# Pooling a CIN kernel's sums over the partitions: four column groups of the array in place of one

## The chip, the cores and the metric

The kernel runs on one core of one Trainium2 chip. The metric is the device time in microseconds; lower is better. The page of the profile shows one execution by itself, whose span runs from its first instruction to its last. Engines go by these names: PE is TensorE (PEld its weight loads), DVE is VectorE, ACT is ScalarE, POOL is GpSimd, SP is SyncE, which here issues transfers only.

## The reference

The input is a batch of 1024 rows, each with 64 fields of 16 numbers. Three layers of a compressed interaction network follow, each a product of every field of the input with every field of the layer before, contracted with a weight matrix; then the sums over the 16 numbers, and one dot product:

```python
for i in range(n):                                   # n = 3
    z = jnp.einsum('bfe,bge->bfge', x0, h)
    z = z.reshape(Bn, f0 * fh, e)
    y = jnp.einsum('oc,bce->boe', Ws[i], z) + bs[i][None, :, None]
    x_i, h = (y[:, :half, :], y[:, half:, :])        # the last layer: (y, y)
    xs.append(x_i)
pooled = jnp.sum(jnp.concatenate(xs, axis=1), axis=2)
return pooled @ fc_w.T + fc_b
```

The result is one number for each row of the batch, 1024 in all.

## The kernel before, in words

The batch is cut into 32 chunks of 32 rows; a chunk has 512 columns (row times number). The final dot product is folded into the weights, so that only two kinds of terms are left for each chunk: a product of two contracted sums (`factors`), and a product of the input with a linear form of it (`x_v0x`). Both are written to a tile `uu`; `sums` has VectorE add each run of 16 columns and puts the result into `acc`, a tile of [128, 2, 16, 32]: 128 partitions, two kinds of sums, 16 pairs of chunks (`NP` is 16), 32 rows of the batch. The even chunk of a pair lies in partitions 0 to 63, the odd one in 64 to 127. What is left is a sum over those 64 partitions and over the two kinds, with a bias added. That is the pooling.

The order of the work is written out by hand, and each engine runs its own instructions in that order. VectorE makes the products `z` (`product`, line 223) from loads that SP issues, TensorE contracts them with the weights (`contract`, line 257; `half_contract`, line 291, for the first four chunks), ScalarE copies half of a contracted sum (line 361), and VectorE multiplies and reduces (lines 362 and 371). Each chunk takes 16 matmuls of 128x128 weights by 512 columns. The last chunk is contracted in two pieces of 256 columns each, with the pooling placed within the second piece, after two of its four groups of four matmuls (lines 699 to 704).

Pooling (lines 630 to 634) is a matmul with `ones`, two columns of weights: one has ones in the upper 64 partitions, the other in the lower 64. So the result `po` has two partitions, one for the even and one for the odd chunks. For the first 15 pairs there are two matmuls of 480 columns, one for each kind, added up in PSUM; for the last pair there are two of 32 columns, the second of which comes after the last sums. `finish` (lines 636 to 638) has ScalarE add the bias `cst` on the way to SBUF and issues a transfer to the output on ScalarE's queue.

The bias is made near the start: lines 196 to 201 multiply the folded weights with the biases of the layers, in two accumulating matmuls of one column whose weights are a column repeated twice, and line 398 adds the last bias in ScalarE. The result has two partitions. Around it stand a few matmuls on zeros[...] (`keep_clock`, line 105), the shifted copies of the input for the first chunks (line 184), and the first contraction.

Of the kernel before, what the change touches and what calls it, by code (L numbers as in the profile page):

```python
# [36 lines left out]
F32 = mybir.dt.float32  # L37
AF = mybir.ActivationFunctionType
ALU = mybir.AluOpType
# [3 lines left out]
E = 16  # L43
B = 1024
CB = 32
# [17 lines left out]
def cin_kernel(ctx, tc, xra, xrb, wh, w0r, w1h, w2t, wx1, wx0, vec, out):  # L63
    nc = tc.nc
# [6 lines left out]
    ps = ctx.enter_context(tc.tile_pool(name="ps", bufs=2, space=bass.MemoryType.PSUM))  # L71
# [3 lines left out]
    def const_tile(name, shape):  # L75
        return const.tile(shape, F32, tag=name, name=name)
# [12 lines left out]
    vs = const_tile("vs", [128, NV])  # L89
    nc.scalar.dma_start(out=vs, in_=vec)  # L90
    fc2, bh1, bh2 = vs[:, 0:1], vs[:, 1:2], vs[0:64, 2:3]
    bcol, fcol, fcb = vs[:, 3:5], vs[:, 5:7], vs[0:2, 7:8]
    w0ds, fcr = vs[:, 8:72], vs[:, 72:200]

    fv2 = const_tile("fv2", [128, 32])
# [5 lines left out]
    misc = ps.tile([128, N], F32, tag="acc", name="misc", bufs=4)  # L101
# [9 lines left out]
    for base in (0, 64, -64):  # L111
        nc.gpsimd.affine_select(
            out=shift, in_=shift, compare_op=ALU.not_equal, fill=1.0, base=base,
# [3 lines left out]
    ones = const_tile("ones", [128, 2])  # L117
# [75 lines left out]
    keep_clock(3)  # L193


    cst = const_tile("cst", [2, 1])
    for j in range(2):
        nc.tensor.matmul(
            misc[0:2, 0:1], fcol[:, j : j + 1].to_broadcast([128, 2]), bcol[:, j : j + 1],
            start=(j == 0), stop=(j == 1),  # L200
        )


    acc = const_tile("acc", [128, 2, NCH // 2, CB])
# [14 lines left out]
    def product(c, j, first=0, last=NI, engine=nc.vector):  # L219
        if first == 0:  # L220
            zs[c, j] = z_tile(f"z_{c}_{j}")
        at = slice(first, last)
        engine.tensor_tensor(  # L223
            zs[c, j][:, at, :], xas[c][:, at, :],
            xbs[c][j].unsqueeze(1).to_broadcast([128, last - first, N]), ALU.mult,
        )
        if j == NJ - 1:
            nc.scalar.activation(zs[c, j][SQ, 0, :], xas[c][SQ, 0, :], AF.Square)  # L228
# [24 lines left out]
    def contract(c, j, piece=0):  # L253
        acc_c, cols = pieces(c)[piece]
        for i in tiles(j):
            t = j * NI + i
            nc.tensor.matmul(  # L257
                acc_c, w_all[:, t, w_cols(c)], zs[c, j][:, i, cols],
                start=(t == 0 and c % 4 < 2), stop=(t == NT - NI and c % 4 >= 2),
            )  # L260
# [90 lines left out]
    def factors(c, which=slice(0, 1)):  # L351

        uu = uu_tile(c // 2)[halves[c % 2], 0, :]
        if c in HEAD:
            at = halves[1 - c % 2]
            nc.vector.tensor_tensor(uu, q_accs[c // 2][at], hb[at, c // 2, :], ALU.mult)
            return
        h = halves[c % 2]
        for acc_c, cols in pieces(c)[which]:
            q = sp.tile([128, N], F32, tag="q", name=f"q_{c}_{cols.start}")  # L360
            nc.scalar.copy(q[h, cols], acc_c[64 - h.start : 128 - h.start])  # L361
            nc.vector.scalar_tensor_tensor(  # L362
                uu[:, cols], acc_c[h], bh1[h], q[h, cols], ALU.add, ALU.mult
            )
# [4 lines left out]
    def sums(k, rows=slice(0, 128), of=slice(0, 2), half=slice(0, CB)):  # L369

        nc.vector.tensor_reduce(  # L371
            acc[rows, of, k, half],
            uus[k][rows, of, E * half.start : E * half.stop].rearrange("p k (b e) -> p k b e", e=E),
            AX.X,
            ALU.add,
        )
# [18 lines left out]
    nc.scalar.copy(w0o[0], w0s[0][:, :, 1, :])  # L395
    h1_weights(0, w0o[0])
    product(c0, 0, 2, NI)
    nc.scalar.activation(cst, misc[0:2, 0:1], AF.Identity, bias=fcb, scale=float(E))
    nc.scalar.copy(w0o[1], w0s[1][:, :, 1, :])
    product(c0, 2)  # L400
    h1_weights(1, w0o[1])
# [31 lines left out]
    for n in range(2):  # L433
        pv = ps.tile([128, 512], F32, tag=("y", "set")[n], name=f"pv2_{n}")
        for k in range(4):
            nc.tensor.matmul(  # L436
                pv[32 * k : 32 * k + 32], fv2, w2s[n][:, k * 512 : (k + 1) * 512],
                start=True, stop=True,
                tile_position=(0, 32 * k),
# [5 lines left out]
    for h in range(2):  # L445
        at = slice(32 * h, 32 * h + 32)
# [30 lines left out]
    def m_ap(f1, f2, dims):  # L477
        return bass.AP(tensor=md.tensor, offset=md.offset + f1 * row + f2 * F, ap=dims)
# [3 lines left out]
    for half, queue in enumerate((nc.sync, nc.scalar)):  # L482
        queue.dma_start(
            out=m_ap(0, 32 * half, [[row, F], [1, 32 * F]]), in_=m_rows[halves[half]]
# [5 lines left out]
        out=m_ap(64, 68, [[row, 4], [4 * F, 7], [1, 4 * F]]),  # L490
        in_=m_rows[0:4, 4 * F :].rearrange("p (k c) -> p k c", c=4 * F),
# [132 lines left out]


    NP = NCH // 2
    res = const_tile("res", [2, NP, CB])
    outs = out.rearrange("(k h b) o -> h k (b o)", h=2, b=CB)

    def pool(pairs, part):  # L630
        nc.tensor.matmul(  # L631
            po[:, pairs, :], ones, acc[:, part, pairs, :],
            start=(part == 1), stop=(part == 0), skip_group_check=True,
        )

    def finish(pairs):
        nc.scalar.activation(res[:, pairs, :], po[:, pairs, :], AF.Identity, bias=cst)
        nc.scalar.dma_start(out=outs[:, pairs, :], in_=res[:, pairs, :])


    order = [4, 5, 6, 7, 2, 3] + list(range(8, NCH))
    first, last = slice(0, NP - 1), slice(NP - 1, NP)
    for s, c in enumerate(order):
        k, head = c // 2, c in HEAD
        if 0 < s < len(order) - 2 and s not in (2, 3):
# [43 lines left out]
            x_v0x(k)  # L689
            sums(k - 1)  # L690

    po = ps.tile([2, NP, CB], F32, tag="set", name="po")


    sums(NP - 1, of=slice(1, 2))
    sums(NP - 1, slice(0, 64), slice(0, 1))
    factors(NCH - 1)
    sums(NP - 1, slice(64, 128), slice(0, 1), slice(0, CB // 2))
    for j in range(NJ):
        if j == 2:  # L700
            pool(first, 1)
            pool(first, 0)
            pool(last, 1)
        contract(NCH - 1, j, 1)
    finish(first)
    factors(NCH - 1, slice(1, 2))
    sums(NP - 1, slice(64, 128), slice(0, 1), slice(CB // 2, CB))
    pool(last, 0)
    finish(last)


# [69 lines left out]
```

## Time and profile before

Three runs took 489.01, 489.15 and 489.27 us; their median is 489.15 us. The run that was profiled took 489.07 us, and its span is 487.3 us, at a full TensorE clock.

| What (profile before) | us |
|---|---|
| span of the profiled execution | 487.3 |
| TensorE matmul busy | 482.3 |
| VectorE busy | 367.6 |
| ScalarE busy | 90.7 |
| pooling matmuls (line 631), 8 records | 2.0 |
| activation of 2x480 in `finish` | 0.65 |
| activation of 2x32 in `finish` | 0.28 |
| issue of the first and the second output transfer | 0.50 and 0.26 |

Busy time is what the records of an engine cover. The records of matmuls overlap each other and their ends are modelled, so TensorE's share says only that it nearly always had a matmul in hand. What is worth reading is the chain of work that ended last: it follows back from the last instruction to what released each step. A group line gives the program's line, the engine, the operation, the tiles written and read, the shapes and the number of records; the bracket at the end of a timeline line gives the idle time ahead of it and what ended that. An f32 matmul leaves two records of weight load and two of matmul.

### The profile page before, as it was taken

Reading aid. Unit: us, or ns where it says so; the run is one execution under the profiler, and the core shown is the slowest. Engines: PE = TensorE matmul, PEld = TensorE weight load, DVE = VectorE, ACT = ScalarE, POOL = GpSimd, SP = SyncE. Lnnn points to the kernel's source line nnn. Section 1 sums busy time; section 2 is a strip of 40 time slices with the busy share of each in tenths; the row PEclk is TensorE's granted clock in tenths of the full one; section 3 lists DMA queues with packets and bytes.
Section 4 is the critical chain, followed back from the end, with each engine's and each line's share of the span. In section 5 each row is a group of like instructions: output and inputs, shape, how many; then the busy total and the mean of one; then the engine's idle time right before and its main releaser. Section 6 shows DMA issues by size and latency. Waiting matters only on the chain.

```text
span 487.3 us, 3939 instructions
## 1 busy us (share of the span) xinstructions
PE 482.3 (99%) x1622; PEld 216.4 (44%) x1622; DVE 367.6 (75%) x229; ACT 90.7 (19%) x158; POOL 16.6 (3%) x15
## 2 busy tenths in 40 slices
PE   9999999999999999999999999999999999999996
PEld 4564344343344344444444344443444434444474
DVE  5993899998899988898777687767868676680311
ACT  3325202022211122212221112212022122010001
POOL 5340000000000000000000000000000000000000
PEclk9999999999999999999999999999999999999999
DMA  8967974442746263544333244433244440000000
GB/s 335 422 250 229 426 299 172 172 172 108 317 178 261 82 263 126 208 182 174 153 116 126 124 172 172 172 140 117 89 172 172 172 172 1 0 0 1 0 0 2
DMA packets 14386, 78.59 MB, mean 161 GB/s; under 512 B 3772, under 2 KB 4444, under 8 KB 5472
## 3 DMA queue, kind: packets, MB, share of 16 engines
q1 hardware_dynamic: 13228, 77.05, 40.1%
q10 hardware_dynamic: 1140, 1.29, 0.9%
q8 instruction: 13, 0.21, 0.2%
q14 instruction: 5, 0.04, 0.0%
HBM read 76.69 MB, written 1.64 MB: 161 GB/s over the span
## 4 chain that ended last, share of the span: by engine, by line
PE 99%; DVE 0%; ACT 0%; issue 0%; POOL 0%; POOLq 0%
PE acc L257 79%; PE acc L291 6%; PE q L330 6%; PE acc L279 3%; PE acc L267 2%; PE xp L184 1%; PE misc L105 1%; PE po L631 0%; PE pm L462 0%; PE pv L436 0%; PE q L279 0%; PE q L341 0%; PE y L284 0%; PE acc L312 0%; DVE uu L362 0%
## 5 line engine op out<-in xcount | busy, mean ns | idle before, releaser
L257 PE MATMUL acc<-z,w_all 128*128 128x512 f32 (+1 forms) x928 | 387.6, 579 | 0.0
L223 DVE TENSOR_TENSOR z<-xa,xb 128x2048 f32<-128x2048 f32 x125 | 281.0, 2285 | 45.9 <-PE acc L257 38.6
L257 PEld LDWEIGHTS acc<-z,w_all 128*128 128x128 f32 x928 | 175.4, 190 | 210.9 <-issue 208.0
L228 ACT ACTIVATE z<-xa 32x512 f32<-32x512 f32 x34 | 21.3, 625 | 324.4 <-DVE z L223 321.9
L362 DVE SCALAR_TENSOR_TENSOR uu<-acc,vs,q 64x512 f32<-64x512 f32 (+1 forms) x29 | 21.2, 731 | 59.9 <-ACT q L361 59.7
L291 PE MATMUL acc<-z,w_all 128*64 128x256 f32 x256 | 28.5, 381 | 0.0
L330 PE MATMUL q<-z,w_all 128*64 128x512 f32 x128 | 27.9, 594 | 0.0
L361 ACT COPY q<-acc 64x512 f32<-64x512 f32 (+1 forms) x29 | 16.4, 565 | 36.5 <-PE acc L257 22.9
L291 PEld LDWEIGHTS acc<-z,w_all 128*64 128x64 f32 x256 | 18.0, 137 | 11.2 <-issue 2.5
L223 DVE TENSOR_TENSOR z<-xa,xp 128x2048 f32<-128x2048 f32 (+2 forms) x10 | 18.1, 1856 | 5.9 <-PE xp L184 5.9
L371 DVE TENSOR_REDUCE acc<-uu 128x64 f32<-128x1024 f32 (+3 forms) x19 | 20.3, 1073 | 0.3
L240 ACT COPY xx<-xa 64x512 f32<-64x512 f32 x32 | 19.6, 613 | 0.5
L236 ACT ACTIVATE sq<-xa 32x512 f32<-32x512 f32 x28 | 17.6, 629 | 0.7
L330 PEld LDWEIGHTS q<-z,w_all 128*64 128x64 f32 x128 | 9.0, 137 | 18.3 <-issue 18.0
L284 PE MATMUL y<-xx,bd 64*64 64x512 f32 x64 | 15.5, 603 | 0.0
L279 PE MATMUL acc<-xx,v1w 64*64 64x512 f32 (+1 forms) x58 | 13.5, 587 | 0.0
L367 DVE SCALAR_TENSOR_TENSOR uu<-y,cx,xx 128x512 f32<-128x512 f32 x16 | 11.4, 746 | 0.3
L223 POOL TENSOR_TENSOR z<-xa,xb_gps 128x2048 f32<-128x2048 f32 x2 | 9.1, 4564 | 5.8 <-ACT xb_gps L387 4.3
L267 PE MATMUL acc<-sq,w_sq 32*128 32x512 f32 (+1 forms) x58 | 8.0, 623 | 0.0
L279 PEld LDWEIGHTS acc<-xx,v1w 64*64 64x64 f32 x58 | 3.6, 132 | 8.9 <-issue 8.8
L223 POOL TENSOR_TENSOR z<-xa,xb 128x2048 f32<-128x2048 f32 x1 | 5.9, 5890 | 13.1 <-DMA xb<-in_xrb 13.1
L184 PE MATMUL xp<-xa,shift 64*64 64x512 f32 x32 | 5.6, 803 | 0.0
(62 smaller groups left out, 65.2 us busy)
## 6 DMA issues: line engine op xcount, KB each, us to landing
xa<-in_xra SPq DMA_DIRECT2D x32, 1024.0 KB, 4.8
xb<-in_xrb SPq DMA_DIRECT2D x31, 1024.0 KB, 6.9
w<-in_w2t SPq DMA_DIRECT2D x2, 1024.0 KB, 10.9
xa<-in_xra SPq DMA_DIRECT2D x2, 768.0 KB, 7.9
w1s<-in_w1h SPq DMA_DIRECT2D x1, 1024.0 KB
w1x<-in_wx SPq DMA_DIRECT2D x1, 1024.0 KB, 9.0
w0x<-in_wx SPq DMA_DIRECT2D x1, 1024.0 KB, 7.2
w0t<-in_w0r SPq DMA_DIRECT2D x1, 768.0 KB, 6.5
```

The lines of the kernel that those rows point to most:

```text
L223: engine.tensor_tensor(zs[c, j][:, at, :], xas[c][:, at, :], xbs[c][j].unsqueeze(1).to_broadcast([128, last - first, N]), ALU.mult,)
L228: nc.scalar.activation(zs[c, j][SQ, 0, :], xas[c][SQ, 0, :], AF.Square)
L236: nc.scalar.activation(sqs[c // 4][at : at + 32], xas[c][0:32, 0, :], AF.Square)
L240: nc.scalar.copy(xxs[c // 2][to], xas[c][to, 0, :])
L257: nc.tensor.matmul(acc_c, w_all[:, t, w_cols(c)], zs[c, j][:, i, cols], start=(t == 0 and c % 4 < 2), stop=(t == NT - NI and c % 4 >= 2),)
L267: nc.tensor.matmul(acc_c, w_sq[at, w_cols(c)], sqs[first // 4][at, cols], start=(r >= 2), stop=(r < 2), tile_position=(32 * r, 0),)
L279: nc.tensor.matmul(acc_c[q], v1w[rows], xxs[k][rows, cols], start=False, stop=(c >= FIRST and c % 4 < 2), skip_group_check=True,)
L291: nc.tensor.matmul(accs[c][halves[n]], w_all[:, t, 0:64], zs[c, j][:, i, n * H2 : (n + 1) * H2], start=(t == 0), stop=False,)
L330: nc.tensor.matmul(q_accs[k][halves[1 - n]], w_all[:, t, 64:128], zs[2 * k + n, j][:, i, :], start=(t == 0), stop=False,)
L361: nc.scalar.copy(q[h, cols], acc_c[64 - h.start : 128 - h.start])
L362: nc.vector.scalar_tensor_tensor(uu[:, cols], acc_c[h], bh1[h], q[h, cols], ALU.add, ALU.mult)
L371: nc.vector.tensor_reduce(acc[rows, of, k, half], uus[k][rows, of, E * half.start : E * half.stop].rearrange("p k (b e) -> p k b e", e=E), ...
```

## The change

Ahead of the pooling, VectorE adds the two kinds of sums of the first 15 pairs in place (128 partitions by 480 numbers). The pooling of these pairs then has one matmul for each quarter of the pairs in place of one for each kind: four pairs (the last quarter three) each, with 128 or 96 columns. Each quarter goes to a column group of the array of its own, so that its result lies in partitions 0, 32, 64 or 96 and the one after it. The last pair still has two matmuls of 32 columns, now in the fourth group. `finish` is called for each quarter and for the last pair: five activations and five transfers in place of two and two, the four of the quarters on SP's queue. As the results lie in several partitions, the bias is made in all 128: the weights of the two matmuls at line 198 are a column repeated 128 times.

```diff
-    bcol, fcol, fcb = vs[:, 3:5], vs[:, 5:7], vs[0:2, 7:8]
+    bcol, fcol, fcb = vs[:, 3:5], vs[:, 5:7], vs[:, 7:8]
...
-    cst = const_tile("cst", [2, 1])
+    cst = const_tile("cst", [128, 1])
     for j in range(2):
         nc.tensor.matmul(
-            misc[0:2, 0:1], fcol[:, j : j + 1].to_broadcast([128, 2]), bcol[:, j : j + 1],
+            misc[:, 0:1], fcol[:, j : j + 1].to_broadcast([128, 128]), bcol[:, j : j + 1],
...
-    nc.scalar.activation(cst, misc[0:2, 0:1], AF.Identity, bias=fcb, scale=float(E))
+    nc.scalar.activation(cst, misc[:, 0:1], AF.Identity, bias=fcb, scale=float(E))
...
+    QP = NP // 4
-    res = const_tile("res", [2, NP, CB])
+    res = const_tile("res", [128, QP, CB])
-    def pool(pairs, part):
+    def pool(k0, k1, part=0, **flags):
+        g, at = k0 // QP, slice(k0 % QP, (k1 - 1) % QP + 1)
         nc.tensor.matmul(
-            po[:, pairs, :], ones, acc[:, part, pairs, :],
-            start=(part == 1), stop=(part == 0), skip_group_check=True,
-        )
+            po[32 * g : 32 * g + 2, at, :], ones, acc[:, part, k0:k1, :],
+            tile_position=(0, 32 * g), skip_group_check=True, **flags,
+        )
-    def finish(pairs):
-        nc.scalar.activation(res[:, pairs, :], po[:, pairs, :], AF.Identity, bias=cst)
-        nc.scalar.dma_start(out=outs[:, pairs, :], in_=res[:, pairs, :])
+    def finish(k0, k1, queue):
+        g, at = k0 // QP, slice(k0 % QP, (k1 - 1) % QP + 1)
+        rows = slice(32 * g, 32 * g + 2)
+        nc.scalar.activation(
+            res[rows, at, :], po[rows, at, :], AF.Identity, bias=cst[rows]
+        )
+        queue.dma_start(out=outs[:, k0:k1, :], in_=res[rows, at, :])
...
-    po = ps.tile([2, NP, CB], F32, tag="set", name="po")
+    po = ps.tile([128, QP, CB], F32, tag="set", name="po")
+    quarters = [(k, min(k + QP, NP - 1)) for k in range(0, NP, QP)]
...
+    done = acc[:, :, 0 : NP - 1, :]
+    nc.vector.tensor_tensor(done[:, 0], done[:, 0], done[:, 1], ALU.add)
     for j in range(NJ):
         if j == 2:
-            pool(first, 1)
-            pool(first, 0)
-            pool(last, 1)
+            for at in quarters:
+                pool(*at, start=True, stop=True)
+            pool(NP - 1, NP, 1, start=True, stop=False)
         contract(NCH - 1, j, 1)
-    finish(first)
+    for at in quarters:
+        finish(*at, nc.sync)
     factors(NCH - 1, slice(1, 2))
     sums(NP - 1, slice(64, 128), slice(0, 1), slice(CB // 2, CB))
-    pool(last, 0)
-    finish(last)
+    pool(NP - 1, NP, start=False, stop=True)
+    finish(NP - 1, NP, nc.scalar)
```

More of the change, by code (lines that the diff above doesn't have):

```diff
@@ L626, in cin_kernel @@
     NP = NCH // 2
-    res = const_tile("res", [2, NP, CB])
+    QP = NP // 4
+    res = const_tile("res", [128, QP, CB])
     outs = out.rearrange("(k h b) o -> h k (b o)", h=2, b=CB)
-    def pool(pairs, part):
+    def pool(k0, k1, part=0, **flags):
+        g, at = k0 // QP, slice(k0 % QP, (k1 - 1) % QP + 1)
         nc.tensor.matmul(
-            po[:, pairs, :], ones, acc[:, part, pairs, :],
-            start=(part == 1), stop=(part == 0), skip_group_check=True,
-        )
-    def finish(pairs):
-        nc.scalar.activation(res[:, pairs, :], po[:, pairs, :], AF.Identity, bias=cst)
-        nc.scalar.dma_start(out=outs[:, pairs, :], in_=res[:, pairs, :])
+            po[32 * g : 32 * g + 2, at, :], ones, acc[:, part, k0:k1, :],
+            tile_position=(0, 32 * g), skip_group_check=True, **flags,
+        )
+    def finish(k0, k1, queue):
[5 more added lines that the diff above has]
+        queue.dma_start(out=outs[:, k0:k1, :], in_=res[rows, at, :])
     order = [4, 5, 6, 7, 2, 3] + list(range(8, NCH))
-    first, last = slice(0, NP - 1), slice(NP - 1, NP)
     for s, c in enumerate(order):
```

## The prediction

> **What bounds the kernel now.** I read the page first: how busy the engines are, and the chain of work that ended last.
>
> ```profile
> span 487.3 us, 3939 instructions
> PE 482.3 (99%) x1622; PEld 216.4 (44%) x1622; DVE 367.6 (75%) x229; ACT 90.7 (19%) x158; POOL 16.6 (3%) x15
> ...
> PE 99%; DVE 0%; ACT 0%; issue 0%; POOL 0%; POOLq 0%
> ```
>
> The chain is TensorE nearly throughout. So a microsecond taken from TensorE's own stream shortens the run, unless another engine then comes late; work added to VectorE or ScalarE costs only where TensorE comes to wait for it. The pooling lies at the end, so I asked for the chain over the last stretch (start, length, what).
>
> ```profile
> 473.83 3.88 PE acc L257 x18
> 477.71 1.76 PE po L631 x6
> 479.47 3.67 PE acc L257 x16
> 483.14 0.02 issue
> 483.16 0.37 ACT q L361
> 483.53 0.03 issue
> 483.56 0.50 DVE uu L362
> 484.06 0.02 issue
> 484.08 0.43 DVE acc L371
> 484.51 0.14 issue
> 484.64 0.23 PE po L631 x2
> 484.88 0.02 issue
> 484.90 0.28 ACT res L637
> ```
>
> The reader is to see two things. The pooling in the middle (L631 x6) costs 1.76 us on the chain, with contraction before and behind it. From 483.14 on there is a fixed serial tail, one engine after another. The timeline of the same stretch shows who is idle around it:
>
> ```profile
> 475.22 0.42 DVE L371 TENSOR_REDUCE acc<-uu 64x16 f32<-64x256 f32 x1
> 477.64 0.09 PEld L631 LDWEIGHTS po<-acc,ones 128*2 128x2 f32 x2 [0.33 <-issue]
> ...
> 478.05 0.08 PEld L631 LDWEIGHTS po<-acc,ones 128*2 128x2 f32 x1 [0.32 <-issue]
> 478.45 0.09 PEld L631 LDWEIGHTS po<-acc,ones 128*2 128x2 f32 x1 [0.32 <-issue]
> ...
> 479.51 0.65 ACT L637 ACTIVATE res<-po,cst 2x480 f32<-2x480 f32 x1 [4.85 <-PE po L631]
> 480.19 0.50 ACTq L638 DMA_DIRECT2D out<-res  x1
> ```
>
> An f32 matmul leaves two records, and the weight loads show one pass of 480 columns each 0.40 us. VectorE is free from 475.64 to 483.56, ScalarE from 480.84 to 483.16, and SP has nothing left to issue but its wait for the last output.
>
> **What the skill says.** "TensorEngine Tiling (Array Packing)", Key Properties: different tiles of the array load weights and multiply in parallel, and a change of tiling mode drains the engine. The trace agrees. Line 436 runs eight f32 matmuls of 128x32 weights by 512 columns, in two rounds of four column groups; its weight loads:
>
> ```profile
> 17.57 0.16 PEld L436 LDWEIGHTS pv<-w,fv 128*32 128x32 f32 x8 [0.39 <-issue]
> 18.03 0.13 PEld L436 LDWEIGHTS pv<-w,fv 128*32 128x32 f32 x4 [0.30 <-issue]
> 18.45 0.13 PEld L436 LDWEIGHTS pv<-w,fv 128*32 128x32 f32 x4 [0.30 <-issue]
> ```
>
> They come in fours, 0.42 to 0.46 us apart, and the next block starts at 19.43. At the pool's rate (0.40 us per 480 columns, so 0.427 per 512) the sixteen records would take 6.83 us in a row; they took 19.43 - 17.57 = 1.86. "TensorE: Matmul & The Clock Gate", The cost: per-tile semaphore tail, gives some 26 ns for each semaphore increment after a packed group; no row here isolates it.
>
> **The change part by part.** All against the profiled span of 487.3 us; that run took 489.07 us, the three timed ones 489.01 to 489.27 (median 489.15), so a difference in the span is carried over unchanged.
>
> 1. *The middle pooling on TensorE.* Before: two matmuls of 480 columns, two passes each, 4 x 0.40 = 1.60; one of 32 columns, 2 x 32 x 0.40/480 = 0.05; the rest of 1.76, 0.11, is the change of mode. After: four matmuls of 128, 128, 128 and 96 columns in four column groups, then the one of 32 in the fourth group. If the groups run together, as in line 436: 2 passes x 128 x 0.40/480 = 0.21, plus 0.05, plus a fixed part. From line 436, 1.86 - 4 x 0.427 = 0.15. Sum 0.42. Bounds: issue alone gives 0.34, as line 198's four records with one column each took 0.17 on the chain, some 0.025 apart with 0.09 of mode change, and ten records at 0.025 plus 0.09 are 0.34. From above 0.55, if the two more semaphore increments (0.05) and a second weight load fall on the path. Taken: 0.42, **a gain of 1.34 us**.
> 2. *The addition on VectorE.* 128 partitions x 480, f32. The nearest rows: 423 ns for 256 elements (line 554) and 2285 ns for 2048 (line 223), so 0.423 + 224 x (2.285 - 0.423)/1792 = 0.66 us. It starts after the reduction that ends at 475.64, so it ends near 476.3; pooling starts at 477.64. TensorE has 1.3 us to spare. Queued behind it on VectorE is only the factor at 483.56. Cost 0.
> 3. *Four activations and the transfers.* 2x480 took 652 ns and 2x32 took 278 ns, so 2x128 is 0.278 + 96 x 0.374/448 = 0.36. Four are 1.4 us: from about 478.2 to 479.7 (with a little between them to 479.9). The ScalarE copy behind them is due at 483.16 - 1.34 = 481.8. Hidden. The four transfers go to SP, whose data loads are over; ScalarE loses one 0.50 us issue. At 0.50 us each, SP is done by about 480.5, over 4 us ahead of the last transfer. Cost 0.
> 4. *The last pooling, activation and transfer.* Same sizes (2 columns of weights, 32 columns, 2x32), at partitions 96 and 97. No edit there has a price: 0, bounds -0.1 to +0.1 for the end-of-program waits on SP, which now stand behind four more transfers.
> 5. *The bias at the start.* Line 198's weights go from 128x2 to 128x128, four loads on the chain at 8.1 us.
>
> ```profile
> 7.19 0.94 PE L105 MATMUL misc<-bd 128*128 128x128 f32 x6
> 8.06 0.24 PE L198 MATMUL misc<-vs 128*2 128x1 f32 x4
> 8.23 0.44 PE L291 MATMUL acc<-z,w_all 128*64 128x256 f32 x2
> ```
>
> "TensorE: Matmul & The Clock Gate", LDWEIGHTS, prices a load by its columns over 1.2 GHz: an estimate of 0.107 us for 128. The trace has no load alone, but line 105's six pairs of a 128-column load and a 128-column matmul fill 0.86 us on the chain, 0.14 each. So four loads are 0.43 to 0.56, plus 0.09 for the change to line 291, less 0.10 for the change from line 105's full-width mode that is no longer made: 0.42 to 0.55 for 0.17 before, **0.25 to 0.38 more** at that place. But TensorE loses time soon after anyhow: line 184's sixteen records take 2.14 us on the chain where four rounds at 0.427 and 0.15 fixed make 1.86, and its weight loads wait there.
>
> ```profile
> 10.77 0.41 DVE L379 TENSOR_TENSOR w_all<-w0t,w0p 128x256 f32<-128x256 f32 x1
> 10.90 0.53 PEld L184 LDWEIGHTS xp<-xa,shift 64*64 64x64 f32 x8 [0.59 <-DVE z L223]
> ```
>
> The second half of these loads waits for VectorE, to about 11.2, which does not wait for line 198. So 0.28 us of the delay is swallowed. The ScalarE activation at line 398 also comes later, but the copy behind it (line 399) waited 0.62 us for a transfer. Net 0 to 0.1; I take 0, upper end 0.25 if the slack is not there.
>
> Sum: -1.34 us; 489.15 - 1.34 = 487.8. The likeliest case's own range is 487.6 (pooling 0.34, 0.1 off the end) to 488.1 (pooling 0.55, 0.15 kept from the start).
>
> **The rivals.** One measurement can tell about 0.2% from no change, 0.98 us.
> - *The groups run one after another.* Then the columns add up: 2 x 480 x 0.40/480 = 0.80, plus 0.05, plus 0.11, 0.97; up to 1.2 with 0.025 us of issue for each of the eight records. Gain 0.56 to 0.79: 488.4 to 488.6, within 0.2%. For it: these groups are short, a pass lasts 0.107 us against the 0.43 of line 436, and all four read 128 rows. Against: line 436 has the same four groups into one bank, four abreast.
> - *The start is not hidden.* If the waits near 11 us move along with the delay, +0.25 to +0.38 stays: 488.1 to 488.2, on the edge. Against: the wait named there is on VectorE, whose work does not hang on the bias.
> - *Slower: the SP transfers end last.* Four issues in a row on SP start near 478.4. SP woke 1.12 us after the last ScalarE issue began at 485.21 (its wait, 90.0 us from 396.3, ended near 486.33), so 0.86 after that issue ended. The new end would let SP wake at 484.99, so the path is SP's from (484.99 - 0.86 - 478.4)/4 = 1.43 us an issue, and slower than before from 1.77. SP's longest issue in this trace took 2.03 us (line 488): that gives 478.4 + 8.1 + 0.86 = 487.4, 1.05 later than before, 490.2. Against: line 638's issue with thirty rows took 0.50, with two 0.26; these have six or eight rows.
>
> **How the numbers follow.** Groups together, start hidden: 0.76. Groups in a row: 0.12. Start not hidden: 0.06. SP last: 0.06. Faster by over 0.2% is 0.74 of the first (0.02 of it ends above 488.17) and half of the third, 0.77; slower is the fourth, 0.06; within is the rest, 0.17. The range goes from 487.5 to 488.5: the first and third cases and half of the second, 0.88 less small edges.
>
> **What will show it.** In the chain after, L631's place before the last sixteen L257 records should hold some 0.4 us for 1.76; 0.9 to 1.2 says the groups queue. The wait of PEld for VectorE near 11 us should shrink from 0.59, and the block of line 291 should still start near 12.3. The addition should end 1 us or more ahead of pooling. The reduction, pooling and activation at the end should keep 0.43, 0.23 and 0.28. SP's last issue should end before 481. I would be wrong above all if mode changes between the narrow groups drained the array, or if a wait inserted between pooling and activation held TensorE.

## The result and the profile after

The changed kernel takes 487.45 us (median of six runs, 487.37 to 487.80) and the kernel before 489.0 (six runs beside them, 488.82 to 489.27): 1.55 us less, a ratio of 0.997 with a 95% interval of 0.9957 to 0.9982. The prediction was 487.8 us, faster. Some executions of either kernel lie 4 to 7 us above the rest (none of these twelve, but in the second session below 7 of 22 of the changed kernel and 3 of 67 of before; none was profiled, and whether the change makes them more frequent stays open), so the medians and spans of the experiments are of the runs under 491 us, while the ratios and their intervals take in every run.

The page after:

```profile
span 486.0 us, 3955 instructions
PE 481.0 (99%) x1626; PEld 216.7 (45%) x1626; DVE 368.4 (76%) x230; ACT 91.5 (19%) x161; POOL 16.3 (3%) x15
```

TensorE's modelled busy time falls by 1.3 us, VectorE gains its one instruction. The chain of the changed kernel over the last stretch (start, length, what):

```profile
472.96 4.96 PE acc L257 x23
477.92 0.34 PE po L633 x4
478.25 3.66 PE acc L257 x16
481.92 0.02 issue
481.94 0.37 ACT q L361
482.31 0.03 issue
482.34 0.50 DVE uu L362
482.84 0.02 issue
482.86 0.43 DVE acc L371
483.29 0.14 issue
483.43 0.23 PE po L633 x2
483.66 0.02 issue
483.68 0.28 ACT res L641
```

Pooling now holds 0.34 us of the chain for 1.76. The contraction behind it has 3.66 for 3.67, and from the end of contraction to the last activation it is 1.76 us in both (481.92 to 483.68, and 483.14 to 484.90). The timeline of the same kernel:

```profile
475.85 0.66 DVE L706 TENSOR_TENSOR acc<-acc 128x480 f32<-128x480 f32 x1
477.85 0.27 PEld L633 LDWEIGHTS po<-acc,ones 128*2 128x2 f32 x10 [0.33 <-issue]
477.85 0.41 PE L633 MATMUL po<-acc,ones 128*2 128x128 f32 x10
...
478.33 1.48 ACT L641 ACTIVATE res<-po,cst 2x128 f32<-2x128 f32 x4 [3.47 <-PE po L633]
478.72 1.36 SPq L644 DMA_DIRECT2D out<-res  x4
481.94 0.36 ACT L361 COPY q<-acc 64x256 f32<-64x256 f32 x1 [2.13 <-PE acc L257]
```

The addition ends at 476.51, 1.34 us before the first weight load. The ten loads of pooling fall within 0.27 us, where before they came one at a time, 0.40 apart. ScalarE's four activations end at 479.81 and SP's last issue at 480.08; ScalarE then waits 2.13 us for contraction.

The profiled span fell by 1.3 us only, less than the 1.42 that pooling gave. The rest is at the start. There the chain of this execution begins with a load's landing:

```profile
0.75 3.22 DMA xa<-in_xra
3.96 0.14 issue
4.10 2.92 PE xp L184 x16
7.01 0.86 PE misc L105 x6
7.88 0.34 PE misc L198 x4
8.22 1.88 PE acc L291 x16
10.10 2.42 PE xp L184 x16
12.52 5.33 PE acc L291 x48
```

The large block of line 291 starts at 12.52, before at 12.31. From there to pooling it is 465.40 us in both, and in every profile taken for this study in which TensorE does not wait there. The start of the block moves from execution to execution: 12.07 to 12.75 in the profiles of this study. Line 198 holds 0.34 us for 0.17 in this chain, and yet experiment 4 shows that this need not make the block late.

### The profile page after: what moved, and what is told of

Its sections match the earlier page's. It is cut to its first block, busy times and chain, and to the rows that moved or that the text cites. A ratio compares the mean times of both kernels' runs of the same rounds, so it can differ in the third digit from the quotient of the medians.

```text
span 486.0 us, 3955 instructions
## 1 busy us (share of the span) xinstructions
PE 481.0 (99%) x1626; PEld 216.7 (45%) x1626; DVE 368.4 (76%) x230; ACT 91.5 (19%) x161; POOL 16.3 (3%) x15
## 4 chain that ended last, share of the span: by engine, by line
PE 98%; DMA 1%; DVE 0%; ACT 0%; issue 0%
PE acc L257 80%; PE acc L291 6%; PE q L330 6%; PE acc L279 3%; PE acc L267 2%; PE xp L184 1%; DMA xa<-in_xra 1%; PE pm L462 0%; PE pv L436 0%; PE q L279 0%; PE q L341 0%; PE misc L105 0%; PE y L284 0%; PE acc L312 0%; PE po L633 0%; DVE uu L362 0%
```

## The experiments

All are timed against the kernel before on the same chip: 489.15 us in the first two sessions, 489.06 in the third. The effects are 0.1 to 0.3% of the run, so the chain of the profile carries each argument, and the timed runs are the check on it.

**1. The addition alone.** One matmul of 480 columns in place of two; no groups, output and bias as before.

```diff
+    nc.vector.tensor_tensor(done[:, 0], done[:, 0], done[:, 1], ALU.add)
...
-            pool(first, 1)
-            pool(first, 0)
-            pool(last, 1)
+            pool(first, 0, start=True, stop=True)
+            pool(last, 1, start=True, stop=False)
```

> The kernel before with one part of the change: VectorE adds the two kinds of sums of the first 15 pairs, and one matmul of 480 columns pools them into two partitions; one activation of 2x480, one transfer on ScalarE's queue, the bias in two partitions. Theory (the gain is TensorE's streaming time in the pooling block, and VectorE's addition is hidden): the block falls from 1.76 us on the chain by one matmul, 2 passes x 0.40, to 0.96; the run by 0.8 us, to about 488.2. Rival (half of the gain came from elsewhere: the shorter activations, SP's queue or the end of the program): the block falls as said and the run by something clearly other than 0.8. Second rival (TensorE waits for the addition): L631's first weight load waits for VectorE and the run gains less than 0.5.

Its chain at pooling:

```profile
477.68 0.95 PE po L631 x4
478.64 3.67 PE acc L257 x16
```

The block lost 0.81 us, one matmul of 480 columns. The runs give a median of 488.50, 0.65 less (488.11 to 489.06; ratio 0.9994, interval 0.998 to 1.0008). The profile agrees with the theory. The times are too scattered to settle 0.65 against 0.81, but the spans of the same runs are not: their mean is 486.55 us for 487.34, 0.79 less. TensorE did not wait for the addition.

**2. The groups alone.** The changed kernel without the addition; each group takes both kinds.

```diff
-    nc.vector.tensor_tensor(done[:, 0], done[:, 0], done[:, 1], ALU.add)
...
-            for at in quarters:
-                pool(*at, start=True, stop=True)
+            for part in (1, 0):
+                for at in quarters:
+                    pool(*at, part, start=(part == 1), stop=(part == 0))
```

> The changed kernel without VectorE's addition: the four column groups each take both kinds of sums, two accumulating matmuls a group, eight in all. Theory (groups run together, so columns of one group alone count): four passes of 128 columns, 4 x 0.107 = 0.43, plus the block's remainder of the changed kernel (0.34 - 2 x 0.107 = 0.13): 0.56 on the chain, a gain of 1.2 us over before and 0.2 lost against the changed kernel: about 487.7. Rival (the addition is the main part): the block stays above 1.0 and the gain under 0.8.

Here the chain cuts the block off a little early (0.50, with 3.71 for the contraction behind it), so I read it from weight load to weight load in the timeline:

```profile
477.92 0.44 PEld L633 LDWEIGHTS po<-acc,ones 128*2 128x2 f32 x18 [0.33 <-issue]
477.92 0.61 PE L633 MATMUL po<-acc,ones 128*2 128x128 f32 x18
478.46 3.32 PEld L257 LDWEIGHTS acc<-z,w_all 128*128 128x128 f32 x16
```

477.92 to 478.46 is 0.54 us, close to the 0.56 expected; read in the same way, before has 1.76 and the changed kernel 0.33. So 1.22 of the 1.43 us come with the groups alone. Median 487.98, 1.17 less than before (ratio 0.9974, 0.9956 to 0.9993). The rival is out. The two parts do not add up (0.81 and 1.22 make 2.03, together they give 1.43), since the groups have already divided by four the columns that the addition would halve: behind the groups it is worth 0.21 us, two passes of 128 columns.

**3. One group for all four quarters.** The matmuls keep their number and size; `po`, `res` and `finish` are fitted to two partitions (not shown).

```diff
-            po[32 * g : 32 * g + 2, at, :], ones, acc[:, part, k0:k1, :],
-            tile_position=(0, 32 * g), skip_group_check=True, **flags,
+            po[:, k0:k1, :], ones, acc[:, part, k0:k1, :],
+            tile_position=(0, 0), skip_group_check=True, **flags,
```

> The changed kernel with the four quarters put through one column group, one after the other, into two partitions; addition, number of matmuls, four activations, SP's four transfers and the bias in 128 partitions stay. Theory (running abreast is what the groups bring): 480 columns x 2 passes = 0.80 plus the pair of 32 (0.05) plus mode change (0.09): 0.95 to 1.15 on the chain, a loss of 0.6 to 0.8 us against the changed kernel: about 488.1. Rival (short matmuls overlap in one group too, as their records do): block near 0.4 and the run as the changed kernel, 487.5.

```profile
477.69 0.97 PE po L632 x10
478.67 3.67 PE acc L257 x16
```

0.97 us, as the prediction worked out for groups in a row, and the median is 488.32 (ratio 0.9989, 0.9975 to 1.0003; mean span 0.85 less than before). The same ten weight loads and ten records take 0.63 us less when they go to four column groups. In the changed kernel the first records of the four groups start within 0.02 us of each other (477.85 to 477.87); here each record of the quarters starts 0.11 us after the one ahead of it, or 0.08 where that one has 96 columns. It is the running abreast, not the number or the length of the matmuls.

**4. The bias alone.** The kernel before with `cst` made in 128 partitions.

```diff
...
-            misc[0:2, 0:1], fcol[:, j : j + 1].to_broadcast([128, 2]), bcol[:, j : j + 1],
+            misc[:, 0:1], fcol[:, j : j + 1].to_broadcast([128, 128]), bcol[:, j : j + 1],
...
```

> The kernel before with the other part alone: the bias made in 128 partitions, weights of 128 columns at line 198; pooling and output as before. Theory (TensorE waits near 11 us anyhow): line 198 takes 0.34 us on the chain for 0.17, the wait of line 184's loads for VectorE shrinks by as much, the second block of line 291 starts as before relative to that VectorE instruction, and the run stays at 489.0 within 0.15. Rival (the delay stays): +0.17 to +0.2 us, the block of line 291 later by that.

Its chain near the start no longer runs over TensorE's early work:

```profile
6.86 0.42 DVE w_all L379
7.28 3.34 DVE z L223 x2
10.62 0.04 issue
10.66 1.41 PE xp L184 x8
12.07 5.33 PE acc L291 x48
```

and the timeline has the wait that swallows the delay (0.59 us before, 0.87 in the changed kernel):

```profile
10.52 0.41 DVE L379 TENSOR_TENSOR w_all<-w0t,w0p 128x256 f32<-128x256 f32 x1
10.66 0.53 PEld L184 LDWEIGHTS xp<-xa,shift 64*64 64x64 f32 x8 [0.98 <-DVE z L223]
...
12.00 1.08 PE L291 MATMUL acc<-z,w_all 128*64 128x256 f32 x7
```

Line 291's block follows the VectorE instruction by 1.48 us here, 1.47 before (10.77 to 12.24) and 1.48 after (10.97 to 12.45). Median 489.15, as before (ratio 0.9993, 0.9982 to 1.0004). The wait did not shrink as expected; it grew, because in this execution TensorE came there early: the last rounds of line 184's first block start 0.43 us apart here, and 0.85 in the profile of before. What held is the point of the theory: VectorE, and what it waits for, set the start of that block, so the wider bias costs nothing.

**5. The addition made late.** Four more additions of its size stand ahead of it.

```diff
+    for _ in range(4):
+        nc.vector.tensor_tensor(spare, done[:, 0], done[:, 1], ALU.add)
     nc.vector.tensor_tensor(done[:, 0], done[:, 0], done[:, 1], ALU.add)
```

> The changed kernel with VectorE's addition made late: four additions of the same size into a spare tile stand ahead of it, each 0.66 us. The addition then ends near 479.15 after the changed kernel's clock, where TensorE comes to pooling at 477.85. Theory (the addition costs nothing because 1.34 us of slack cover it): TensorE waits 1.3 us at the first weight load of L633, and the run gets 1.3 us longer than the changed kernel, near 488.9. Rival (the weight load is ordered so that contraction goes on meanwhile, or VectorE's additions overlap): less than 0.6 longer.

```profile
476.09 2.73 DVE L708 TENSOR_TENSOR spare<-acc 128x480 f32<-128x480 f32 x4
478.86 0.66 DVE L709 TENSOR_TENSOR acc<-acc 128x480 f32<-128x480 f32 x1
479.57 0.27 PEld L633 LDWEIGHTS po<-acc,ones 128*2 128x2 f32 x10 [1.82 <-DVE acc L709]
479.57 0.40 PE L633 MATMUL po<-acc,ones 128*2 128x128 f32 x10 [1.42 <-DVE acc L709]
```

TensorE waits 1.42 us; four additions start 0.69 apart, 2.77 in all, less 1.34 of slack. So the slack is real, and work beyond it goes straight to the path. The run is longer than that: a median of 489.52, 1.9 more than the changed kernel (ratio to before 1.0047, 1.0021 to 1.0073). Its spans have a median of 487.4 for 485.8, 1.6; the other 0.3 lies outside the span, and no record tells why.

**6. The four transfers on ScalarE's queue.**

```diff
-        finish(*at, nc.sync)
+        finish(*at, nc.scalar)
```

> The changed kernel with the four quarters' transfers issued by ScalarE instead of SP. Theory (ScalarE has 3.6 us between the first quarter's activation and the copy for the last piece): four activations at 0.36 and four issues at 0.24 to 0.5 take 2.4 to 3.4 us, the copy still starts when contraction ends; the run stays at 487.6 within 0.15. Rival (SP's queue is part of the gain): 0.2 or more longer.

487.62 us (487.50 to 487.71), 1.44 less than before; ratio 0.9969, 0.9957 to 0.9981. ScalarE's last of the four issues ends at 481.10, 0.67 us ahead of the copy at 481.77. SP's queue is not part of the gain. The changed kernel again, in the second session:

> The changed kernel itself, beside the next three on the same chip. Theory (start of the work depends on when the first loads land, the rest is fixed): 487.5 to 487.7; in the profile the stretch from the second block of line 291 (the one of 48 records) to the pooling is 465.40 us as in all profiles so far, and the block of L633 holds 0.34 us on the chain. Rival (the first measurement was a lucky one): a gain under 1.2 us against before.

A median of 487.63, 1.52 less than before, and a mean span 1.50 less. The ratio of all runs, 0.9995 (0.997 to 1.0019), does not settle it by itself. The profile has 0.34 us for pooling again, and 465.40 from the block of line 291 (12.35) to it (477.75).

**7. Three attempts at better: pooling behind the last contraction.** TensorE waits there for 1.5 us anyhow. First with two groups:

```diff
-    QP = NP // 4
+    QP = NP // 2
...
     for j in range(NJ):
-        if j == 2:
-            for at in quarters:
-                pool(*at, start=True, stop=True)
-            pool(NP - 1, NP, 1, start=True, stop=False)
         contract(NCH - 1, j, 1)
-    for at in quarters:
-        finish(*at, nc.sync)
+    for at in quarters:
+        pool(*at, start=True, stop=True)
+    pool(NP - 1, NP, 1, start=True, stop=False)
     factors(NCH - 1, slice(1, 2))
+    for at in quarters:
+        finish(*at, nc.sync)
```

> A version meant to be better: the pooling of the first 15 pairs stands behind the last contraction in place of within it, where TensorE waits for ScalarE, VectorE and the last sums for 1.5 us; in two column groups of 256 and 224 columns, with two activations behind the ScalarE copy and two transfers on SP. Theory: 2 x 0.213 + 0.05 + 0.09 is about 0.57 us of pooling in a wait of 1.5, so the 0.34 us and the slow second weight load behind it (0.1) leave the chain; ScalarE's two activations (0.47 and 0.44) end about 1.3 us after contraction, the last one is due at 1.75. A gain of 0.34 to 0.45 over the changed kernel, near 487.1. Rival (ScalarE or the transfers come late at the end): no gain or a loss up to 0.5.

Then with the four groups of the change:

> The same move with four column groups: pooling is shorter, but four activations (3 x 0.36, 0.33, with some 0.03 between them) stand between ScalarE's copy and its last activation: they end 0.37 + 1.5 = 1.9 us after contraction, where the last one is due at 1.75. Theory (ScalarE is now the bound in the tail): the last activation starts 0.1 to 0.2 us late, a gain of 0.2 to 0.3 over the changed kernel, less than with halves. Rival (TensorE's share alone counts): the same gain as with halves or more.

And, without groups, one matmul of 480 columns, moved the same way:

> VectorE's addition, and one matmul of 480 columns moved behind the last contraction, one activation of 2x480 behind ScalarE's copy, its transfer on SP; no column groups, bias in two partitions. Theory (the place matters, not the groups: TensorE has 1.5 us of waiting there): pooling takes 0.95 of the wait, the activation runs 1.05 to 1.70 us after contraction and the last one is due at 1.76, so the end of contraction to the last activation stays at 1.8 and the run gains 0.3 to 0.45 over the changed kernel, 487.2 to 487.3. Rival (the end is lengthened by ScalarE's late activation, by its transfer, or by the closing steps, as with the two moved versions): 487.5 or more.

None gained what was expected. The medians are 487.55 us with two groups (0.08 below the changed kernel of that session; ratio to before 1.0009, 0.9984 to 1.0034), 488.58 with four (0.95 above it; 0.9997, 0.9975 to 1.002) and 487.55 with one matmul (0.9968, 0.9956 to 0.9981). The chain of the first:

```profile
473.97 7.34 PE acc L257 x34
481.31 0.57 PE po L633 x4
481.88 0.02 issue
481.91 0.46 ACT res L641
482.37 0.03 issue
482.40 0.45 ACT res L641
482.84 0.04 issue
482.89 0.23 PE po L633 x2
```

Contraction now runs through in 7.34 us, and what was expected of TensorE came: measured from the start of line 291's block, ScalarE's copy behind contraction starts 0.53 us sooner in all three than in the second profile of the changed kernel. That is more than the 0.34 us of pooling. Contraction's matmuls start 0.216 us apart; over the pooling block in the changed kernel one such step takes 0.64 us and the next 0.32, so the block costs contraction 0.53 us in all, and 1.96 in the kernel before.

The gain is lost behind contraction, in two stretches:

| us | changed kernel, second profile | two groups | four groups | one matmul |
|---|---|---|---|---|
| start of ScalarE's copy to the last activation | 1.74 | 1.80 | 2.19 | 1.92 |
| issue of the last transfer to the end of the span | 2.03 | 2.33 | 2.89 | 2.27 |

In the first stretch the last pooling waits until ScalarE has read the same PSUM tile (its wait in the trace ends with ScalarE's activation); with four activations ScalarE is the chain there for 1.48 us. The second stretch is the close of the program. With two groups the last transfer lands 1.07 us after its issue, as in the changed kernel, and the rest comes behind the landing: SP has more transfers left to wait for (0.33 us to its first closing drain for 0.21), and from that drain to the end it is 0.93 us for 0.75. One of ScalarE's closing drains falls there, which takes 135 ns with two groups and 136 with one matmul, for 8 in the changed kernel; why it is longer is not shown. With four groups that drain is short again (8 ns), and the loss is in the landing: the last transfer lands 1.88 us after its issue for 1.07. In that execution one instruction fetch of 8 KB began at 484.32 and took 0.50 us, and the second of the two output packets came 0.45 us behind the first. Whether the fetch delayed it is not shown; what sets the close was not tried.

## Why the prediction was right

- *TensorE bounds the end of the kernel.* Right: in every profile in which pooling was shortened in place, all behind it moved by as much.
- *The middle pooling, 1.76 to 0.42.* Right in kind, a little too dear: 0.34. The sum was 0.21 for the two passes of 128 columns, 0.05 for the last pair's matmul of 32, and 0.15 fixed, from line 436. The slip is the 0.05. The last pair follows in the fourth group, whose own quarter has 96 columns, so this group too streams 128 columns twice, beside the others: its records start at 477.87, 477.95, 478.03 and 478.06, and the next weight load of contraction comes at 478.18. Without the 0.05, 0.13 is left as the fixed part. The lower bound, from issue alone, was 0.34 too, but that is chance: the records of the fourth group start as far apart as their columns take (0.08 for 96), not 0.025. That the groups run abreast, as the Trainium skill says ("TensorEngine Tiling (Array Packing)", Key Properties) and line 436 showed for long matmuls, holds for passes of 0.1 us too; experiment 3 gives the price of the rival, 0.97 as worked out.
- *The semaphores.* The Trainium skill ("TensorE: Matmul & The Clock Gate", The cost: per-tile semaphore tail) gave some 26 ns an increment. The prediction kept it for the upper bound, for two more increments. The trace has fewer: one in the whole block after, on its last record, for two before. So no run here shows the price.
- *The addition, 0.66 us at no cost.* 0.66 measured, with 1.34 us to spare for 1.3. Experiment 5 spent the slack.
- *Activations and transfers.* 1.48 us for 1.4, and 0.24 to 0.28 for an SP issue where 0.50 was assumed. Hidden; experiment 6 shows that the queue is indifferent. The slower rival needed 1.43 us an issue to touch the path. (ScalarE was free from 480.69, where its first issue ends, not from 480.84; nothing hangs on it.)
- *The end.* 2.02 us from the last issue to the end of the span for 2.08: within the bounds of 0.1. ScalarE's issue itself took 0.48 us for 0.26, which the prediction had not foreseen; the transfer still landed 1.07 us after the start of its issue, as before.
- *The bias.* 0.34 us for an expected 0.42 to 0.55. The loads were priced rightly: they start 0.11 us apart, so four are 0.45 for 0.43 to 0.56. Too small was the change of mode that is no longer made: from the last weight load of line 105 to the first of line 198 it is 0.31 us before and 0.11 after, so 0.20 is saved for the 0.10 taken. The delay is hidden, as said. What the prediction had wrong besides is the sign of one mark: the wait near 11 us did not shrink but grew, from 0.59 to 0.87. VectorE came 0.20 us later (10.97 for 10.77), behind the load of `xa` at the head of the chain after; TensorE came 0.07 earlier (10.03 for 10.10), in spite of this load and of line 198, since line 184's first block takes 2.92 us for 3.33: the rounds of its matmuls start 0.85 us apart at first and 0.43 later, and the point where this changes differs from execution to execution. The prediction did not foresee it; it did no harm, as VectorE sets the start of the large block.
- *The sum.* 1.34 forecast, 1.55 measured in the timed runs, 1.42 by the chain. 0.06 more is the close; the last 0.07 is within the scatter of single runs (before: 488.82 to 489.27). The 487.45 us lie just under the stated 487.5 to 488.5, as before ran 0.15 us faster beside it than the 489.15 that the prediction starts from; as a gain, 1.55 lies within the 0.65 to 1.65 of that range, near its upper end.

## What to carry to other kernels

When one engine is the chain, look for matmuls in its stream with few columns of weights: here four of them, in column groups side by side, took about what one of them takes. Halving the streamed columns with an addition on another engine and dividing them among column groups share the same microseconds, so their gains must not be added. An idle stretch near the end is no free place: what is moved there brings its followers along (activation, transfer, closing steps), and these had less slack than TensorE.

## What was not expected of the hardware

A block of pooling costs the contraction around it more than its own place on the chain: 0.53 us for a block of 0.34, and 1.96 for one of 1.76. Moving it past the last contraction lengthened the close of the program by 0.2 to 0.3 us with two activations or one, and by 0.9 with four, though the last transfer was issued no later: 471.0 to 471.4 us after the start of line 291's large block, for 471.5 in the changed kernel's second profile.
